# Sorted rows of each image's first half turned by loads and VectorE, image 0's second pair loaded sooner, and two calls of the step loop in another order

## The chip, the cores and the metric

The kernel runs on one core of one Trainium2 chip. A core has five engines that work side by side: TensorE (matrix products; PE in the profile, its weight loads listed apart as PEld), VectorE (DVE), ScalarE (ACT), GpSimd (POOL) and SyncE (SP, which here only starts transfers). Each takes its instructions strictly in the order in which the program lists them for it, and waits on semaphores that other engines or landed transfers raise. Transfers between on-chip memory and HBM are started from a queue (SP's, ACT's or GpSimd's) and carried by 16 DMA engines. The metric is device time in microseconds (us) of one execution; less is better.

## The reference, cut to what matters

x is [4, 32, 128, 128] in f32: four images, regrouped into 128 channels (c) of 4096 pixels (i, j).

```python
# layer 0, for each image: attention between all pairs of pixels
energy = jnp.einsum('bci,bcj->bij', q, q)                      # 4096 x 4096, symmetric
d = jnp.sqrt(jnp.diagonal(energy, axis1=1, axis2=2))
attn = jax.nn.softmax(energy / (d[:, :, None] * d[:, None, :]), axis=-1)
x = gamma * jnp.einsum('bcj,bij->bci', q, attn) + xs           # then put back to image order
# layer 1, on each image's 4096 tokens of 128
t = t + linear_attention(layernorm(t))
n = layernorm(t)
p = softmax(n @ router_w + router_b)                           # 8 experts
top_p, top_i = top_k(p, 2); top_p = top_p / sum(top_p)
t = t + sum_k top_p[k] * (n @ expert_w[top_i[k]] + expert_b[top_i[k]])
```

## The kernel before, in words

**Attention of layer 0 (`attend`).** The 4096 pixels of an image are 8 chunks of 512. Because the energy is symmetric, only the tiles with chunk `jc` <= chunk `i` are computed: a loop over rows `i`, in it over tiles `jc`, in it over four sub-tiles `j` of 128. One turn of the inner loop is a *step*: a product `pe` (L609), its exponential `pr` on ScalarE (L612), and, two steps later, the product `po` (L497, `values`) that multiplies `pr` into the row's output. The tile's mirror image is needed as well. VectorE transposes `pr` in 32x32 blocks into a tile `F` (L421 is the line under which the profile lists it), the queue SP writes F to DRAM (`move`, L530) and reads it back with its groups swapped (`bring`, six transfers, L545), and later four products `pg` (L433, `transposed_share`; L453 for tiles on the diagonal) add it to the other chunk's output. So a usual step on TensorE is pe, po, pg: six instructions of 128x512, since an f32 product takes two.

**What sets the order.** All of it is written out by hand, for TensorE, VectorE, ScalarE and SP. `after(n, f)` puts f in a list that `turn_tick` runs n steps later. `clock` counts TensorE work in units of 128 columns: 2*(CH-c0)/P for a step's pe and po (8 for a full one), 4 for a share. `bring` appends a share to the list `late` with the clock value `clock + LAG` (57) at which it is due, and `step_share` runs one part of the first share that is due. At the end of each step stand `turn_tick()`, then `clock += ...`, then `step_share()`. In the first tile of a row, at j == 2, turn_tick runs the row's first `po`, which needs the accumulator that ScalarE has just copied out for the row before (L502).

**Other work, spread between the steps.** Generators are advanced between steps: `timed` ones at shares of an image's clock (loads and normalisation of the next image's chunk pairs, `prep`), and a `steady` one at most once in 10 clock units (`layer1` of the image before, during `attend` of the next one). A step of the steady generator is two yields.

**The sorted experts (`sorted_experts`, images 0 to 2).** Each half of an image's tokens (h = 0 and 1) is written by GpSimd's indirect transfers to DRAM rows `xs[h]` of 132 values (128 channels and the token's weight), sorted by expert and padded to NT = 39 tiles of 128 rows, each tile of one expert. Then for pairs of tiles (20 of them, one pair in a step): `load` brings the rows to on-chip buffers (SP, L1096); three steps later TensorE turns them with two transposes (L1137) into PSUM, ScalarE copies them out (L1106), in the next step TensorE multiplies them by the expert's matrix, whose place is a register (L1130, two instructions for each tile), VectorE scales the result by the token's weight (L1112), and SP writes it to `ys` (L1116). GpSimd gathers from `ys` afterwards.

**The start.** `prep_first` loads image 0's chunks 0 and 1 (`load_quarters`, L308, into the one buffer `xx`), turns them on VectorE (L316), squares and sums them (L295, L296), takes the power -1/2 on GpSimd (L164), scales (L338), and TensorE transposes them (ptn, L344) into `qn`. `prep(0, 1)` does chunks 2 and 3 in another form: its factors `wide` (L388) are transposed on TensorE (pnorm, L399), and VectorE scales with them. Its load uses the same buffer `xx`.

**The end.** Image 3's layer 1 runs after its attention (`last_parts`).

## Time and profile before

Three runs took 1651.45, 1651.85 and 1653.72 us: the median is 1651.85. The profiled execution took 1650.83 us, with a span of 1649.0 us of instructions and a granted TensorE clock of 0.996.

| What | busy us | share of the span | instructions |
|---|---|---|---|
| TensorE | 1609.9 | 98% | 5192 |
| its weight loads | 846.5 | 51% | 5192 |
| VectorE | 931.5 | 56% | 2383 |
| ScalarE | 898.5 | 54% | 2839 |
| GpSimd | 593.8 | 36% | 565 |

| Group | count | busy us | mean ns of one |
|---|---|---|---|
| po, L497 | 1152 | 549.4 | 559 |
| pe, L609 (128x512, two inputs) | 896 | 458.8 | 594 |
| pg, L433 | 880 | 449.8 | 593 |
| transposes of sorted rows on TensorE, L1137 | 234 | 45.2 | 273 |
| expert products, L1130 | 468 | 71.6 | 275 |
| copies of the turned rows, ScalarE, L1106 | 120 | 45.2 | 377 |
| scaled results, VectorE, L1112 | 120 | 49.9 | 416 |

A busy time is the union of the instructions' spans, and the duration of one matmul holds its way through the array as well: neighbouring matmuls overlap, and what one costs is the distance between the starts of two in a row. The DMA engines moved 345.37 MB in 304297 packets, on average 209 GB/s.

### The profile page before, as it was taken

What the parts mean: (1) busy time and instruction counts of PE and PEld (TensorE: products, weight loads), DVE (VectorE), ACT (ScalarE), POOL (GpSimd) and SP (SyncE); (2) the same over time, 40 slices, a digit from 0 to 9 for tenths busy, and PEclk for the clock granted to TensorE, in tenths of its full rate; (3) what the DMA queues carried; (4) which work ended last, traced back from release to release, by engine and by line L of the source; (5) the groups of instructions that cost most, each with busy time, mean ns of one, the idle gap of its engine ahead of it and who ended that gap; (6) DMA issues with size and microseconds to landing.
All of it is one profiled execution on the core that took longest, in us unless ns stands there. A gap on an engine that the chain in (4) does not pass through costs nothing.

```text
span 1649.0 us, 21309 instructions
## 1 busy us (share of the span) xinstructions
PE 1609.9 (98%) x5192; PEld 846.5 (51%) x5192; DVE 931.5 (56%) x2383; ACT 898.5 (54%) x2839; POOL 593.8 (36%) x565
## 2 busy tenths in 40 slices
PE   8999999999999999999999999999999999999987
PEld 4444544455554455555554455555554455555633
DVE  4543353567586443549478443448658634345786
ACT  3555445466475555547556455556656555545386
POOL 1000000001015441446555543256555652437166
PEclk9999999999999999999999999999999999999999
DMA  4655656676759777997899777798699877886001
GB/s 143 205 179 178 197 187 213 222 231 204 168 196 283 239 222 220 266 257 200 211 221 287 253 236 241 222 268 230 196 209 279 275 248 236 248 251 192 14 14 39
DMA packets 304297, 345.37 MB, mean 209 GB/s; under 512 B 82096, under 2 KB 230704, under 8 KB 289840
## 3 DMA queue, kind: packets, MB, share of 16 engines
q1 hardware_dynamic: 269712, 304.50, 59.9%
q0 software_dynamic: 26624, 25.58, 7.6%
q10 hardware_dynamic: 7840, 13.93, 2.9%
q8 instruction: 44, 0.72, 0.2%
q14 instruction: 77, 0.63, 0.1%
HBM read 167.08 MB, written 182.09 MB: 212 GB/s over the span
## 4 chain that ended last, share of the span: by engine, by line
PE 81%; DVE 7%; DMA 5%; ACT 3%; SPq 2%; issue 1%; POOL 1%; ACTq 0%; DVEq 0%; POOLq 0%
PE po L497 24%; PE pe L609 23%; PE pg L433 20%; PE pys L1130 3%; PE py L1304 3%; PE pg L453 2%; PE pys L1137 2%; PE pgram L725 2%; DMA F<-blocks 1%; DVE F L421 1%; DMA blocks<-rows 1%; SPq L938 1%; ACT pr L612 1%; ACT xn L696 1%; DMA blocks<-F 1%
## 5 line engine op out<-in xcount | busy, mean ns | idle before, releaser
L612 ACT ACTIVATE pr<-pe 128x512 f32<-128x512 f32 (+1 forms) x576 | 322.4, 560 | 547.5 <-PE pe L609 507.0
L497 PE MATMUL po<-pr,qT 128*128 128x512 f32 (+3 forms) x1152 | 549.4, 559 | 4.2 <-ACT o L502 3.9
L609 PE MATMUL pe<-qn,qn 128*128 128x512 f32 x896 | 458.8, 594 | 4.6 <-ACT pr L612 4.6
L433 PE MATMUL pg<-F,qT 128*128 128x512 f32 x880 | 449.8, 593 | 4.7 <-DMA F<-blocks 4.7
L421 DVE STREAM_TRANSPOSE F<-pr 128x512 f32<-128x512 f32 x440 | 305.4, 700 | 134.5 <-ACT pr L612 124.7
L497 PEld LDWEIGHTS po<-pr,qT 128*128 128x128 f32 x1152 | 215.2, 190 | 250.2 <-issue 217.9
L1178 POOL DMA_INDIRECT acc<-ys,place x128 | 202.1, 1579 | 209.1 <-ACT pr L612 134.8
L438 ACT ACTIVATE junk<-F 128x512 bf16<-128x512 f32 x440 | 273.0, 620 | 4.9 <-DMA F<-blocks 4.9
L433 PEld LDWEIGHTS pg<-F,qT 128*128 128x128 f32 x880 | 166.8, 190 | 199.4 <-issue 182.3
L1066 POOL DMA_INDIRECT xs<-xn,place x192 | 186.0, 969 | 184.1 <-ACT pr L612 118.9
L609 PEld LDWEIGHTS pe<-qn,qn 128*128 128x128 f32 x896 | 155.6, 191 | 119.1 <-issue 106.7
L442 DVE TENSOR_TENSOR o<-o,pg 128x512 f32<-128x512 f32 x110 | 75.1, 683 | 205.4 <-PE pg L433 205.2
L1112 DVE TENSOR_TENSOR results<-pys,xn 128x256 f32<-128x256 f32 x120 | 49.9, 416 | 187.2 <-ACT xn L1106 168.5
L164 POOL TENSOR_TENSOR rn<-ss,neg_half 128x8 f32<-128x8 f32 (+1 forms) x17 | 27.2, 1602 | 320.0 <-DVE ss L296 319.9
L612 ACT ACTIVATION_READ_ACCUMULATOR pr<-pe 128x1 f32 x576 | 111.9, 194 | 0.0
L1106 ACT ACTIVATE xn<-pys 128x256 f32<-128x256 f32 x120 | 45.2, 377 | 111.4 <-PE pys L1137 111.4
L1130 PEld LDWEIGHTS pys<-ew_sb,xn 128*128 128x128 f32 x468 | 70.5, 191 | 52.2 <-issue 49.7
L609 PE MATMUL pe<-qn 128*128 128x512 f32 (+3 forms) x256 | 91.4, 440 | 0.7 <-ACT qn L342 0.7
L1178 POOL DMA_INDIRECT yb<-ys,place x64 | 60.8, 950 | 81.1 <-DMA F<-blocks 31.1
L438 ACT ACTIVATION_READ_ACCUMULATOR junk<-F 128x1 f32 x440 | 84.5, 192 | 0.0
L1130 PE MATMUL pys<-ew_sb,xn 128*128 x468 | 71.6, 275 | 0.0
L1304 PE MATMUL py<-ew_sb,xn 128*128 128x512 f32 x128 | 61.5, 622 | 5.1 <-ACT tmp L1260 3.9
(217 smaller groups left out, 1463.2 us busy)
## 6 DMA issues: line engine op xcount, KB each, us to landing
blocks<-F SPq DMA_DIRECT2D x110, 1024.0 KB
F<-blocks SPq DMA_DIRECT2D x220, 192.0 KB
F<-blocks SPq DMA_DIRECT2D x220, 128.0 KB
xn<-xs SPq DMA_DIRECT2D x114, 132.0 KB
ys<-results SPq DMA_DIRECT2D x114, 128.0 KB
F<-blocks SPq DMA_DIRECT2D x220, 64.0 KB
below<-F SPq DMA_DIRECT2D x31, 384.0 KB
T<-in_x_dram SPq DMA_DIRECT2D x64, 128.0 KB
```

Of the source, the lines that this page charges most:

```text
L421: f()
L433: nc.tensor.matmul(pg.rearrange("p (a f) -> p a f", a=4), st["qT"][i][:, ib, :], G[:, :, ib], start=(ib == 0), stop=(ib == NJ - 1),)
L438: nc.scalar.activation(junk, G[:, :, ib], AF.Copy, accum_out=st["sums"][:, NJ * i + ib, jc : jc + 1])
L442: nc.vector.tensor_tensor(st["o"][jc], st["o"][jc], pg, ALU.add)
L497: nc.tensor.matmul(row["po"][:, lo:hi], qT[blk // NJ][:, blk % NJ, :], w, start=start, stop=(row["left"] == 0))
L609: nc.tensor.matmul(pe[:, c0:], qn[jc][:, ts(j, P)], qn[i][:, c0:], start=True, stop=True)
L612: nc.scalar.activation(pr[:, c0:], pe[:, c0:], AF.Exp, accum_out=sums[:, t, i : i + 1]).ins
L1066: inst = nc.gpsimd.indirect_dma_start(xs[h], offset(place[:, i, k : k + 1]), xn[:, k, :], None)
L1112: nc.vector.tensor_tensor(result[:, :n], p[:, 2 * P : 2 * P + n * D].rearrange("p (j c) -> p j c", c=D), bufs[g % 6][:, :n, D : D + 1].to_ ...
L1130: nc.tensor.matmul(p[:, 2 * P + j * D : 2 * P + j * D + D], bufs[6 + g % 2][:, j, :D], weights[:, bass.ds(begins[2 * (g % 2) + j], D)], st ...
L1178: inst = nc.gpsimd.indirect_dma_start(to, None, ys, offset(place[:, i, k : k + 1]), compute_op=op)
L1304: nc.tensor.matmul(bank, xn[:, k, :D], ew_sb[:, 4 * h : 4 * h + 4, :], start=True, stop=True)
```

## The change

**1. First halves.** For h == 0 the rows of a quad of four tiles are loaded by four transfers (one for each 32 channels) that place the 32x32 blocks so that VectorE's blockwise transpose of 128x512 gives the turned rows. TensorE's transposes and ScalarE's copies are gone for this half; TensorE multiplies the four tiles of a quad together, and one VectorE instruction scales them. The weights come by a transfer of their own (`factor`). All buffers are parts of this half's `xn`: two for loads, two for turned rows. The second half (h == 1) is as before.

**2. Image 0's second pair.** It is loaded into a buffer of the pool `work` and no longer into `xx`, directly after the first pair's load and before the tokens `T`. Its four turns stand between the instructions of `prep_first`, whose order on VectorE is now written out, with the first half's sums ahead of the second half's.

**3. The step loop.** `clock` is raised before the two calls, for every step; in the first tile of a row at j == 2, `step_share` runs ahead of `turn_tick`.

**4.** `prep` has one more yield ahead of pnorm for image 0.

```diff
         rows = st["T"][:, ts(kc, 8), :]
         return rows.rearrange("p k (w r) -> p k w r", r=2)
 
-    def load_quarters(b, kc, queues=(nc.sync, nc.sync)):
-
-        xa = xin.tile([P, 2, 2, 2, HW2, 2], F32, tag="xx", name=f"xa_{b}_{kc}")
+    def load_quarters(b, kc, queues=(nc.sync, nc.sync), place=(xin, "xx")):
+
+        xa = place[0].tile([P, 2, 2, 2, HW2, 2], F32, tag=place[1], name=f"xa_{b}_{kc}")
         halves = x[b].rearrange("c (s g) w -> c s (g w)", s=2)
         for a in (0, 2, 1, 3):
             first_row = 16 * kc + 4 * a
...
             )
         return xa
 
+    def turn_quarter(s, k, xa, qT):
+        nc.vector.transpose(
+            qT[:, s, 2 * k : 2 * k + 2, :].rearrange("p h (e r c) -> p r (h e) c", e=2, r=2),
+            xa[:, s, k].rearrange("p r (h t) e -> p (r h) e t", h=2),
+        )
+
     def turn_quarters(s, xa, qT):
         for k in range(2):
-            nc.vector.transpose(
-                qT[:, s, 2 * k : 2 * k + 2, :].rearrange("p h (e r c) -> p r (h e) c", e=2, r=2),
-                xa[:, s, k].rearrange("p r (h t) e -> p (r h) e t", h=2),
-            )
+            turn_quarter(s, k, xa, qT)
 
     def prep_first(st):
 
...
         yield
         ss = stat.tile([P, 2 * NJ], F32, tag="ss", name=f"ss_{b}_{kc}")
         rn = stat.tile([P, 2 * NJ, 1], F32, tag="rn", name=f"rn_{b}_{kc}")
-        for s in range(2):
+        def rows_squared(s):
             turn_quarters(s, xa, qT)
-            squares(b, kc, s, qT, ss)
+            sq = work.tile([P, NJ, P], F32, tag="qs", name=f"sq_{b}_{kc}_{s}", bufs=2)
+            nc.vector.tensor_tensor(sq, qT[:, s], qT[:, s], ALU.mult)
+            return sq
+
+        def summed(s, sq):
+            nc.vector.tensor_reduce(ss[:, ts(s, NJ)], sq, AX.X, ALU.add)
             pow_neg_half(rn[:, ts(s, NJ), 0], ss[:, ts(s, NJ)])
-        keep_running(40, ps_g, "pg")
-        scaled = []
-        for s in range(2):
-            qs = work.tile([P, NJ, P], F32, tag="qs", name=f"qs_{b}_{kc}_{s}", bufs=2)
+
+        def scale_rows(s):
+            qs = work.tile([P, NJ, P], F32, tag="grp", name=f"qs_{b}_{kc}_{s}", bufs=2)
             nc.vector.tensor_tensor(qs, qT[:, s], rn[:, ts(s, NJ)].to_broadcast([P, NJ, P]), ALU.mult)
             scaled.append(qs)
+
+        scaled = []
+        keep_running(40, ps_g, "pg")
+        summed(0, rows_squared(0))
+        sq = rows_squared(1)
+        st["turns"].pop(0)()
+        scale_rows(0)
+        summed(1, sq)
+        st["turns"].pop(0)()
+        st["turns"].pop(0)()
+        scale_rows(1)
+        st["turns"].pop(0)()
         for s, qs in enumerate(scaled):
             qn = channels(b, kc, s, st)
             pt, done = hold(f"ptn_{b}_{kc}_{s}", lambda p, qn=qn: nc.scalar.activation(qn, p, AF.Copy))
...
 
 
 
-        ahead = 2 if b == 0 and kc == 1 else 5
-        xa = load_quarters(b, kc)
+        soon = b == 0 and kc == 1
+        ahead = 2 if soon else 5
+        if soon:
+            xa = load_quarters(b, kc, place=(work, "wide"))
+            yield
+        else:
+            xa = load_quarters(b, kc)
         if b == 0:
             load_tokens(st["T"][:, ts(kc, 8), :], b, 8 * kc, 8)
             xx = rows_of_image(b, kc, st)
-        for _ in range(ahead):
-            yield
         qT = chunks_of(b, kc, st)
-        for s in range(2):
+        if soon:
+            st["turns"] = [partial(turn_quarter, s, k, xa, qT) for s in range(2) for k in range(2)]
+            yield
+        for _ in range(0 if soon else ahead):
+            yield
+        for s in range(0 if soon else 2):
             turn_quarters(s, xa, qT)
             yield
         if b > 0:
...
         for s in range(2):
             nc.vector.tensor_copy(wide[:, :, s], rn[:, ts(s, NJ)].to_broadcast([P, NJ, 64]))
         yield
-        if b:
-            yield
+        yield
 
         def scale_all(bank):
             for s in range(2):
...
                     elif jc == i and j in (1, 2):
 
                         after(1 if j == 2 and order[-1] == i else 2, partial(below, own, (2, 1) if j == 1 else (3,)))
-                    turn_tick()
                     clock[0] += 2 * (CH - c0) // P
-                    step_share()
+                    steps = (turn_tick, step_share)
+                    for step in reversed(steps) if jc == order[0] and j == 2 else steps:
+                        step()
                     yield
 
     def finish():
...
                         nc.tensor.transpose(p[:, ts(j, P)], bufs[g % 6][:, j, :D], ident)
                 return done
 
+            room = xn[:, half, :].rearrange("p k w -> p (k w)")
+            parts = [room[:, 4 * DW * i : 4 * DW * i + 4 * D] for i in range(4)]
+            quads = [(g, min(4, NT - 4 * g)) for g in range((NT + 3) // 4)]
+
+            def read(inst):
+                wait_for(inst.ins, xs_made[h], "a tile holds tokens of any row")
+                xs_read[h].append(inst.ins)
+
+            def load_blocks(g, n):
+                rows = xs[h][4 * g * P : (4 * g + n) * P, :D].rearrange("(m i) w -> i m w", i=S)
+                for q in range(4):
+                    read(
+                        nc.sync.dma_start(
+                            parts[g % 2][ts(q, S), : n * D].rearrange("i (m c) -> i m c", c=S), rows[:, :, ts(q, S)]
+                        )
+                    )
+
+            def turn(g, n):
+                nc.vector.transpose(parts[2 + g % 2][:, : n * D], parts[g % 2][:, : n * D])
+
+            def four_products(factor, g, n):
+
+                def leave(p):
+                    result = keep["results"].rearrange("p g j c -> p (g j) c")[:, ts(g % 2, 4)]
+                    nc.vector.tensor_tensor(
+                        result[:, :n], p[:, : n * D].rearrange("p (j c) -> p j c", c=D),
+                        factor[:, 4 * g : 4 * g + n].to_broadcast([P, n, D]), ALU.mult,
+                    )
+                    nc.sync.dma_start(
+                        ys[4 * g * P : (4 * g + n) * P, :].rearrange("(j p) d -> p j d", p=P), result[:, :n]
+                    )
+
+                p, done = hold(f"pys_{b}_{h}_{g}", leave)
+                _, begins = nc.values_load_multi_w_load_instructions(
+                    begin[0:1, h, 4 * g : 4 * g + n], engines=[mybir.EngineType.PE], min_val=0,
+                    max_val=(E - 1) * D,
+                    skip_runtime_bounds_check_because="D times a count of at most E - 1, never negative",
+                )
+                weights = ew_sb.rearrange("p e c -> p (e c)")
+                for j in range(n):
+                    nc.tensor.matmul(
+                        p[:, ts(j, D)], parts[2 + g % 2][:, ts(j, D)],
+                        weights[:, bass.ds(begins[j], D)], start=True, stop=True,
+                    )
+                return done
+
+            def turned_by_vector():
+
+                factor = stat.tile([P, NT, 1], F32, tag="factor", name=f"factor_{b}_{h}", bufs=1)
+                read(nc.sync.dma_start(factor, xs[h].rearrange("(t p) w -> p t w", p=P)[:, :, D : D + 1]))
+                leaves = {}
+                for at in range(4 * len(quads) + 10):
+                    for first_at, act in (
+                        (8, turn), (0, load_blocks), (11, partial(four_products, factor)), (13, lambda g, n: leaves.pop(g)()),
+                    ):
+                        if at >= first_at and (at - first_at) % 4 == 0 and (at - first_at) // 4 < len(quads):
+                            g, n = quads[(at - first_at) // 4]
+                            made = act(g, n)
+                            if first_at == 11:
+                                leaves[g] = made
+                    yield
+
             if "results" not in keep:
                 keep["results"] = work.tile([P, 4, 2, D], F32, tag="df", name=f"results_{b}", bufs=1)
-            done = None
             begins = []
-            for at in range(len(pairs) + 5):
-                if at < len(pairs):
-                    load(*pairs[at])
+
+            def turned_by_tensor():
+
+                done = None
+                for at in range(len(pairs) + 5):
+                    if at < len(pairs):
+                        load(*pairs[at])
+                    if done:
+                        done()
+                    yield
+                    turned, applied = (pairs[at - d] if 0 <= at - d < len(pairs) else None for d in (3, 4))
+                    done = products(turned, applied) if turned or applied else None
+                    yield
                 if done:
                     done()
-                yield
-                turned, applied = (pairs[at - d] if 0 <= at - d < len(pairs) else None for d in (3, 4))
-                done = products(turned, applied) if turned or applied else None
-                yield
-            if done:
-                done()
+
+            yield from (turned_by_tensor if h else turned_by_vector)()
             if h == 1:
                 st["sorted"] = True
             yield from idle(1)
...
     UNITS = 3 * NJ * NJ * NCH * (NCH - 1) // 2 + 7 * NJ * NCH
 
     first, second = prep_first(states[0]), prep(0, 1, states[0])
-    next(first)
-    load_weights()
+    ordered = ExitStack()
     next(first)
     next(second)
+    load_weights()
+    ordered.enter_context(tc.manual_schedule(engines=ENGINES))
+    next(second)
+    next(first)
     load_tokens(states[0]["T"][:, 0:8, :], 0, 0, 8)
-
-    ordered = ExitStack()
-    ordered.enter_context(tc.manual_schedule(engines=ENGINES))
-    timed = [(first, 0, 1, 2), (second, 0.5, 5.5, 10)]
+    next(second)
+    next(second)
+    timed = [(first, 0, 1, 2), (second, 1.3, 5.5, 8)]
     for b in range(B):
 
         if b == 0:
```

More of the change, by code (lines that the diff above doesn't have):

```diff
@@ L356, in prep @@
             xx = rows_of_image(b, kc, st)
-        for _ in range(ahead):
+        qT = chunks_of(b, kc, st)
+        if soon:
+            st["turns"] = [partial(turn_quarter, s, k, xa, qT) for s in range(2) for k in range(2)]
             yield
-        qT = chunks_of(b, kc, st)
-        for s in range(2):
+        for _ in range(0 if soon else ahead):
+            yield
+        for s in range(0 if soon else 2):
             turn_quarters(s, xa, qT)
```

## The prediction

> **What bounds the kernel now.** First the page's busy times and the chain that ended last:
>
> ```profile
> PE 1609.9 (98%) x5192; PEld 846.5 (51%) x5192; DVE 931.5 (56%) x2383; ACT 898.5 (54%) x2839; POOL 593.8 (36%) x565
> PE 81%; DVE 7%; DMA 5%; ACT 3%; SPq 2%; issue 1%; POOL 1%; ACTq 0%; DVEq 0%; POOLq 0%
> ```
>
> TensorE sets the time: what leaves its queue or its gaps is gained, unless another engine comes to hold it up. But a busy share is no price, so next I read TensorE's timeline inside a first half's expert products (start, length, instruction, count):
>
> ```profile
> 601.98 0.61 PE L1130 MATMUL pys<-ew_sb,xn 128*128 x4
> 602.42 0.38 PE L1137 MATMUL pys<-ident,xn 128*128 128x128 f32 x2
> 602.64 1.02 PE L609 MATMUL pe<-qn,qn 128*128 128x512 f32 x2
> 603.50 1.02 PE L497 MATMUL po<-pr,qT 128*128 128x512 f32 x2
> ```
>
> Starts tell the price: two transposes take 602.42 to 602.64, so 0.11 us each, as each of the four product instructions does ((602.42 - 601.98)/4); two of 128x512 take 0.86. By these distances TensorE loses only some 62 us of the span in gaps: 10 in the first 50 us, 20 after 1500, and 31 between, of three kinds here. A start wait, a row start and a late F:
>
> ```profile
> 19.73 0.38 PE L497 MATMUL po<-pr,qT 128*128 128x128 f32 x2
> 22.50 0.66 PE L399 MATMUL pnorm<-ident,wide 128*128 128x128 f32 x4 [2.39 <-DVE wide L388]
> 570.49 1.02 PE L609 MATMUL pe<-qn,qn 128*128 128x512 f32 x2
> 571.70 1.13 PE L497 MATMUL po<-pr,qT 128*128 128x512 f32 x2 [0.18 <-ACT o L502]
> 572.66 1.02 PE L433 MATMUL pg<-F,qT 128*128 128x512 f32 x2
> 850.92 1.10 PE L433 MATMUL pg<-F,qT 128*128 128x512 f32 x2 [1.79 <-DMA F<-blocks]
> ```
>
> A gap is longer than its bracket, since the pipeline drains too: po would have started at 570.49 + 0.86 = 571.35, so 0.35 is lost at this row start. Nineteen row starts lose 0.35 (three of them 0.67): 7.2 us. The late F's are three: 1.16 us at 184, 1.95 at 851, 2.04 at 1240. Last the room of the others, by stage (stretch, length, busy time of PE, PEld, DVE, ACT, POOL; clock, DMA share, GB/s):
>
> ```profile
> 583.00:640.00 57.00, 57.00 (x213) 32.00 (x212) 23.37 (x44) 29.82 (x91) 21.31 (x23) 1.00 0.73 226
> 640.00:720.00 80.00, 79.82 (x290) 44.12 (x289) 35.27 (x70) 41.22 (x128) 29.65 (x19) 1.00 0.89 246
> ```
>
> The first is a first half, the second mostly the second half beside the gathers. TensorE loses nothing in the first, and next to nothing at a DMA share of 0.89.
>
> **What the Trainium skill says.** "TensorE: Matmul & The Clock Gate", Part 4: PE-mode transpose, gives about 275 ns for a 128x128 transpose in a kernel. The trace's 273 ns agree as a duration, but the 0.11 us between starts is the cost. "VectorE: DVE Perf Modes", The three transpose paths: VectorE turns 32x32 blocks only; hence the load that places the blocks. The kernel does this already (L950, 128x512: 0.70 us). "DMA: Bandwidth & Descriptors", Specifications: below 512 B a transfer isn't at line rate. The trace's 128 B packets took 15.2 ns in the mean and its 528 B ones 32.2: half the rate.
>
> **The change part by part.** *First halves, TensorE.* Three images x 39 transposes x 0.11 = 12.9 us less; the 117 products stay, and the register loads are as many. ScalarE loses 60 copies of 0.377 (22.6 us): worth nothing by itself, ScalarE has room. VectorE gets 30 turns x 0.70 = 21 us, and 30 scalings of 128x512 (nearest row, L442, 0.683: 20.5) for 60 of 0.416 (25): +5.5 us in each stretch of 57 with 23.4 busy. TensorE's 57 us cover it; uncovered it would cost those 5.5 a half.
>
> *First halves, transfers.* A half has 4992 rows. Before: 4992 packets of 528 B x 32.2 = 161 us of one DMA engine; after: 19968 of 128 B x 15.2 = 303, and 4992 four-byte weights (nearest: the trace's 4 B packets, 10.8 ns: 54). That is +196, or 12.2 us of all sixteen: the share of 0.73 becomes about 0.94. SP's issue times (min/median/max ns):
>
> ```profile
> L938 SPq DMA_DIRECT2D blocks<-rows x48: 557/744/3385, 413.5 to 1228.8; - x48
> L1096 SPq DMA_DIRECT2D xn<-xs x120: 338/424/2255, 571.4 to 1465.6; - x120
> ```
>
> The new loads have 512 pieces each, between 256 (L1096) and 1024 (L938). A quad costs SP 4 x (0.42 to 0.74) + one store of 0.39 = 2.1 to 3.4 us, before 2 x 0.42 + 2 x 0.39 = 1.6. Four steps (two quads, 6.04 us each: 5.16 for pe, po, pg twice and 0.88 for eight products) also hold one F (2.7 + 0.4): SP is then busy for 7.3 to 9.9 of 12.1 us. F has room: in this stretch it landed, by its 2 KB packets, 9 us or more before its share.
>
> The new wait is VectorE's turn on its load. Behind it in the queue stand the F transposes, scalings and sums; late F transposes hold the six pr buffers, then the exponentials, then pe. The load buffers are two, so load g+2 starts when turn g is done, and must land by turn g+2, 12.1 us later: issue at most 3, landing some 3 to 5 (F's own: about 3 after its last issue), being queued behind an F 0 to 3. That makes 6 to 11 us, so it fits, with 1.5 steps more ahead of the product. I charge 1.5 us in all for bursts (bounds: a gain of 0, as pr's six buffers may swallow all; a loss of 25, the rival below).
>
> *The start.* The second pair's load waits today for the first pair's turns (SP's four start at 7.67). Now it stands right behind the first's: started from about 2.1 to 4.6, landed 3.3 later (the first pair: last start 2.35, turned at 5.62), so at 7.9, wanted at about 8.8. VectorE's sum of the first half stands ahead of the second half's turns: 8.21 becomes 7.6, rn 9.71 becomes 9.1, ptn 0.5 us earlier. Then VectorE: scale, sum, two turns (11.3), scale at 11.75 to 12.45, turn, two squares and two sums (2.7) to 15.5, GpSimd's power 1.6, wide 0.5: 17.7, where pnorm's turn on TensorE comes at 19.4. The gap ahead of pnorm (22.50 - 19.95 = 2.55) goes. Sum 3.0; bounds 0 (load late, each us late also delays the scale in front of TensorE's first product) and 3.5 (the added yield may remove a smaller pnorm gap of 0.4).
>
> *The step loop.* Raising clock first means that `bring` reads a value 8 higher: each share falls due one step (1.72 us of pe and po, with 8 units) later. In the changed order of TensorE's instructions this undoes the swap: in rows 3 to 7 of every image no share is due at j == 2 any more, it comes at j == 3. Only rows 1 and 2 of images 1 to 3 have a share ahead of their first po, and these six lost nothing before. So the swap itself is worth 0. The delay is worth more: the late F's of 1.16, 1.95 and 2.04 shrink by 1.72 each, 4.6 us. F is held a step longer, of six buffers some five in use. Four row starts (row 7 of images 1 and 2, row 0 of 2 and 3) get products between the old row's last po and the new one's first: 1.0 us. From image 3's last row, fourteenth step on, TensorE's order is unchanged, and image 2's second half ends four steps earlier before it, so the end keeps its length.
>
> *Sum.* 1650.83 (profiled, span 1649.0) - 12.9 - 3.0 - 4.6 - 1.0 + 1.5 = 1630.8; the median of the runs stands 1.0 above the profiled execution: 1632.
>
> **The rivals.** *Swap works as labelled*, or bursts cost nothing and the end gets shorter: up to 7.2 - 1.0 more, 1625. For it: the gaps are there; against it: the order. *Only the transposes pay*: the second pair lands late, other late F's replace the old: 1652 - 12.9 + 1.5 = 1641. For it: DMA at 0.94. *No change*: what TensorE sheds comes back as waits, 1651; against it: distances of 0.11 are seen in full while nothing waits. *Slower*: the load loop. Place: VectorE's turn in first halves. If turn g to turn g+2 takes longer than 12.1 us, VectorE falls behind by the excess 5 times a half, 15 times in all, and nothing absorbs a steady excess. 20 us of gains are gone at 20/15 = 1.4 us over, a loop of 13.5 us; at 15 us it costs 43 us: 1675. For it: share 0.94, SP near 80%, F loads ahead in the same queue; against it: the 0.89 stretch without gaps, and my 6 to 11 us.
>
> **How the numbers follow.** Forecast 0.69 (own range 1627 to 1637); only transposes, or the loop just touched (1637 to 1647) 0.12; swap works (1622 to 1627) 0.08; no change 0.03; slower (1656 to 1690) 0.08. Range 1625 to 1643. A measurement tells 0.2%, 3.3 us, from no change: faster 0.89, same 0.03, slower 0.08.
>
> **What would show it.** Right: 117 transposes on TensorE instead of 234; starts 0.11 apart in the products; pnorm without a gap; row starts in rows 3 to 7 still losing 0.35; gaps from late F gone at the old places; VectorE's turns waiting for loads only here and there. Wrong: TensorE idle released by VectorE's turned rows or by ScalarE's exponentials in the first halves, F later than its share there, or the start later because the first scale waits for the second pair.

## The result, and the profile after

The changed kernel takes 1643.57 us (median of 6 runs, 1640.39 to 1646.9), the kernel before 1651.28 on the same chip (1649.4 to 1653.72): a ratio of 0.9953, with a 95% interval of 0.9941 to 0.9965. That is 7.7 us faster; the forecast was 20 us, and the time lies just above the top of the range, 1643. The profiled execution took 1644.21 us, its span 1642.4, 6.6 less than the span before.

The page's busy times and the chain that ended last, of the changed kernel:

```profile
PE 1600.1 (97%) x5075; PEld 834.0 (51%) x5075; DVE 945.8 (58%) x2383; ACT 877.3 (53%) x2779; POOL 592.7 (36%) x565
PE 81%; DVE 8%; DMA 4%; ACT 2%; SPq 2%; issue 1%; POOL 1%; ACTq 0%; DVEq 0%; POOLq 0%
```

117 instructions have left TensorE, which still sets the time. But its busy time fell by 9.8 us (from 1609.9) and the span by only 6.6 (from 1649.0): it does less, and waits more. In the chain VectorE has 8% for 7% before; that is a hint, no more, since the page gives whole points.

Next, the expert products of a first half. TensorE's timeline (start, length, instruction, count):

```profile
600.00 1.06 PE L1207 MATMUL pys<-ew_sb,xn 128*128 x8
600.89 1.02 PE L635 MATMUL pe<-qn,qn 128*128 128x512 f32 x2
```

No transpose stands between the products any more, and 8 product instructions take 600.00 to 600.89, the same 0.11 each. The stages of that stretch (busy time of PE, PEld, DVE, ACT, POOL; clock, DMA share, GB/s):

```profile
583.00:640.00 57.00, 57.00 (x193) 30.54 (x192) 30.76 (x52) 24.78 (x79) 18.00 (x20) 1.00 0.92 258
640.00:720.00 80.00, 80.00 (x284) 43.69 (x283) 36.55 (x71) 42.11 (x130) 37.28 (x24) 1.00 0.88 242
```

The DMA share rose from 0.73 to 0.92 and VectorE's work from 23.4 to 30.8 us, and TensorE loses nothing to either. At the start, pnorm:

```profile
19.75 0.38 PE L523 MATMUL po<-pr,qT 128*128 128x128 f32 x2
19.98 0.60 PE L425 MATMUL pnorm<-ident,wide 128*128 128x128 f32 x4
20.41 1.02 PE L635 MATMUL pe<-qn,qn 128*128 128x512 f32 x2
```

The gap of 2.55 ahead of it is gone. So the 12 us that are missing lie elsewhere. The groups of TensorE's instructions give the lead (busy and mean; after the last bar the idle time ahead of the group, and who ended it):

```profile
L523 PE MATMUL po<-pr,qT 128*128 128x512 f32 (+3 forms) x1152 | 549.8, 559 | 2.9 <-ACT o L528 2.9
L635 PE MATMUL pe<-qn,qn 128*128 128x512 f32 x896 | 459.1, 594 | 8.6 <-ACT pr L638 8.6
L459 PE MATMUL pg<-F,qT 128*128 128x512 f32 x880 | 449.6, 592 | 2.0 <-DMA F<-blocks 1.9
L798 PE MATMUL pbd<-ident,rdx 128*128 128x128 f32 x64 | 9.9, 277 | 5.6 <-DVE rdx L776 5.5
```

The same four in the kernel before:

```profile
L497 PE MATMUL po<-pr,qT 128*128 128x512 f32 (+3 forms) x1152 | 549.4, 559 | 4.2 <-ACT o L502 3.9 <-DMA F<-below 0.2 <-DMA F<-blocks 0.2
L609 PE MATMUL pe<-qn,qn 128*128 128x512 f32 x896 | 458.8, 594 | 4.6 <-ACT pr L612 4.6
L433 PE MATMUL pg<-F,qT 128*128 128x512 f32 x880 | 449.8, 593 | 4.7 <-DMA F<-blocks 4.7
L771 PE MATMUL pbd<-ident,rdx 128*128 128x128 f32 x64 | 9.6, 273 | 0.1
```

The row starts (po) and the late F's (pg) lose less, as forecast. New are 5.5 us in which pbd waits for VectorE's rdx, and 4.0 more in which pe waits for ScalarE's exponentials.

The same account in full, by the distances between starts, as the prediction counted: each matmul is priced at its own back-to-back distance (0.429 us for 128x512, 0.110 for 128x128), and what a distance exceeds that is lost. All in us, with the number of gaps; the last three columns are experiments told below. The first two columns are traces from one chip, the last three from two others, where the kernel before took 1653.8, 1653.8 and 1650.8 us for 1651.3 here.

| | before | after | step loop alone | old step order | LAG 49 |
|---|---|---|---|---|---|
| matmuls at their own distance | 1584.7 | 1571.8 | 1584.7 | 1571.8 | 1571.8 |
| lost up to 26 us | 9.4 | 6.8 | 8.1 | 5.4 | 5.3 |
| row starts | 7.2 (18) | 5.2 (14) | 5.2 (14) | 7.2 (18) | 0.4 (1) |
| shares with a late F | 5.2 (3) | 2.1 (1) | 2.8 (2) | 3.6 (3) | 7.6 (3) |
| pbd waits for rdx | 0 | 6.3 (5) | 6.8 (5) | 0 | 0 |
| pe waits for pr | 5.1 (3) | 9.5 (5) | 9.0 (5) | 5.1 (3) | 5.1 (3) |
| matmuls at about double distance | 0 | 1.5 | 3.2 | 0 | 1.5 |
| other gaps over 0.25 | 1.3 | 1.3 | 4.0 | 2.3 | 2.2 |
| gaps under 0.25 | 6.3 | 7.9 | 7.9 | 6.5 | 4.9 |
| from 1500 us on | 20.1 | 20.2 | 19.8 | 18.6 | 18.7 |
| span (with 9.8 outside the matmuls) | 1649.0 | 1642.4 | 1661.4 | 1630.3 | 1627.5 |
| stretches at half clock: up to 26 us, between, from 1500 us on | 1, 0, 2 | 1, 1, 2 | 0, 2, 1 | 0, 0, 1 | 0, 1, 1 |

From before to after: 12.9 of transposes, 2.6 at the start, 3.1 of late F's and 2.0 of row starts are gained, 20.6 together, very nearly the forecast; and 6.3 + 4.3 + 1.5 + 1.6 = 13.7 are lost in four rows in which the forecast had no loss.

The last row counts the stretches of 3.41 us in which the trace has a granted clock of 0.50, without the one that ends every trace. In the middle they are the matmuls at double distance. At the start one costs about 1.4 us with the same code: 6.8 against 5.4 (changed kernel, old step order), 9.4 against 8.1 (before, step loop alone). So the old order's and LAG 49's smaller losses up to 26 us are no gain of theirs, and those from 1500 us on may not be one either. What decides on such a stretch stands in the last section.

**Where pbd waits.** It turns 1/sum of an image's rows, and stands a fixed number of yields behind den (the sums) and rdx, which VectorE makes. The kernel before at the end of image 1 (timeline):

```profile
770.09 0.82 PE L453 MATMUL pg<-F,qT 128*128 128x256 f32 x4
771.42 2.77 DVE L372 TENSOR_TENSOR qn<-xx,pnorm 64x512 f32<-64x512 f32 x4
774.23 0.23 DVE L744 TENSOR_REDUCE den<-sums 128x8 f32<-128x72 f32 x1
774.73 0.78 DVE L749 TENSOR_SCALAR rdx<-rd,gam 128x256 f32<-128x256 f32 x2
776.13 0.60 PE L771 MATMUL pbd<-ident,rdx 128*128 128x128 f32 x4
```

The changed kernel at the same place:

```profile
767.03 0.82 PE L479 MATMUL pg<-F,qT 128*128 128x256 f32 x4
767.35 2.76 DVE L399 TENSOR_TENSOR qn<-xx,pnorm 64x512 f32<-64x512 f32 x4
770.13 0.87 DVE L810 BATCH_NORM_STATS2 bs_a<-T 128x6 f32<-128x128 f32 x4
772.62 0.56 DVE L488 TENSOR_TENSOR o<-o,pg 128x384 f32<-128x384 f32 x1
773.09 0.22 DVE L771 TENSOR_REDUCE den<-sums 128x8 f32<-128x72 f32 x1
773.58 0.62 DVE L776 TENSOR_SCALAR rdx<-rd,gam 128x256 f32<-128x256 f32 x2
774.25 0.66 PE L798 MATMUL pbd<-ident,rdx 128*128 128x128 f32 x4 [1.67 <-DVE rdx L776]
```

The first line of each is the last share that the image's rows wait for. Before, it ended ahead of the next image's scaling (L372), den came right behind that scaling, and rdx was ready at 775.51, with 0.6 us to spare. After, the share comes two of the short steps at a row's end later in TensorE's order, the scaling only one: the share's sum on VectorE (L488) and with it den have slid behind the scaling (L399), the statistics of other rows (L810), six small operations and a transpose. VectorE works without a pause from 765.3 to 774.2. TensorE on the other hand has less between the share and pbd, and would have reached pbd at 772.41 (774.25 less the gap of 1.84).

**Where pe waits.** ScalarE's normalising (L723) stands in its queue ahead of an exponential, and waits for GpSimd's nbo, which waits for VectorE's statistics. The kernel before has this wait too (timeline):

```profile
1261.18 1.02 PE L609 MATMUL pe<-qn,qn 128*128 128x512 f32 x2
1262.99 1.65 ACT L696 ACTIVATE xn<-T,nbo,rsf 128x128 f32<-128x128 f32 x4 [3.81 <-POOL nbo L692]
1265.26 1.12 PE L609 MATMUL pe<-qn,qn 128*128 128x512 f32 x2 [1.56 <-ACT pr L612]
```

The changed kernel:

```profile
1255.13 1.02 PE L635 MATMUL pe<-qn,qn 128*128 128x512 f32 x2
1255.66 1.67 POOL L164 TENSOR_TENSOR rsf<-dm_f,neg_half 128x8 f32<-128x8 f32 x1 [6.12 <-DVE sv_f L715]
1257.70 0.27 POOL L719 TENSOR_SCALAR nbo<-nbf 128x8 f32<-128x8 f32 x1
1258.00 1.65 ACT L723 ACTIVATE xn<-T,nbo,rsf 128x128 f32<-128x128 f32 x4 [3.81 <-POOL nbo L719]
1259.56 0.57 ACT L638 ACTIVATE pr<-pe 128x512 f32<-128x512 f32 x1
1260.27 1.38 PE L635 MATMUL pe<-qn,qn 128*128 128x512 f32 x2 [2.40 <-ACT pr L638]
1261.44 1.91 PE L523 MATMUL po<-pr,qT 128*128 128x512 f32 x2
```

ScalarE idles for 3.81 us in both, with an exponential behind the wait. But its normalising comes 2.87 us after TensorE's last pe, before 1.81 us; TensorE stops for 2.57 us, before for 1.72, and then goes at half clock (the two of po take 1.71 from start to start instead of 0.86). The stop near 872 has grown in the same way, from 1.72 to 2.58. Two more stops, of 1.32 and 1.52 us near 840 and 1228, are new: ScalarE's wait for nbo there was 1.27 and 0.87 us and is 4.68 and 4.85. These four make up the 4.3 us (a fifth stop, near 486, shrank by 0.2). The link from the shares to these statistics isn't followed instruction by instruction here; that the shares' due time makes the loss is what the experiments show. The Trainium skill, "TensorE: Matmul & The Clock Gate", Part 1, says that ScalarE and VectorE take their queues strictly in order; this case agrees, for the exponential at 1259.56 stood behind those 3.81 us.

### The profile page after: what moved, and what is told of

Its sections match the earlier page's. It is cut to its first block, busy times and chain, and to the rows that moved or that the text cites. A ratio compares the mean times of both kernels' runs of the same rounds, so it can differ in the third digit from the quotient of the medians.

```text
span 1642.4 us, 20931 instructions
## 1 busy us (share of the span) xinstructions
PE 1600.1 (97%) x5075; PEld 834.0 (51%) x5075; DVE 945.8 (58%) x2383; ACT 877.3 (53%) x2779; POOL 592.7 (36%) x565
## 4 chain that ended last, share of the span: by engine, by line
PE 81%; DVE 8%; DMA 4%; ACT 2%; SPq 2%; issue 1%; POOL 1%; ACTq 0%; DVEq 0%; POOLq 0%
PE po L523 24%; PE pe L635 23%; PE pg L459 20%; PE py L1398 3%; PE pg L479 2%; PE pys L1207 2%; PE pys L1157 1%; PE pgram L752 1%; DMA F<-blocks 1%; SPq L965 1%; DVE F L447 1%; DVE bs_f L989 1%; PE pys L1164 1%; DMA acc<-t 1%; ACT xn L723 1%
## 5 line engine op out<-in xcount | busy, mean ns | idle before, releaser
L723 ACT ACTIVATE xn<-T,nbo,rsf 128x128 f32<-128x128 f32 x128 | 54.1, 494 | 38.7 <-POOL nbo L719 38.7
L1139 DVE TENSOR_TENSOR results<-pys,xn 128x256 f32<-128x256 f32 (+1 forms) x60 | 24.9, 415 | 82.5 <-ACT xn L1133 71.2
L164 POOL TENSOR_TENSOR rsa<-dm_a,neg_half 128x8 f32<-128x8 f32 x16 | 26.5, 1654 | 117.1 <-DVE sv_a L715 117.0
L164 POOL TENSOR_TENSOR rsf<-dm_f,neg_half 128x8 f32<-128x8 f32 (+1 forms) x15 | 26.2, 1750 | 114.0 <-DVE sv_f L715 114.0
```

The costliest lines, as they stand in the source:

```text
L164: pinned(nc.gpsimd.tensor_tensor(dst, src, neg_half.to_broadcast(list(src.shape)), ALU.pow))
L723: nc.scalar.activation(xn[:, k, :D], T[:, k, :], AF.Identity, scale=rs[:, k, :], bias=nb[:, k, :])
```

## The experiments

The theory (A): part 3, the step loop, raises the clock ahead of turn_tick, so that every share falls due 8 units, one step, late. The late F's gain by it, but the closing work of an image, which needs the shares, and VectorE's and ScalarE's queues behind it lose more. The main rival (B): the turned first halves disturb what comes after them. All times are compared with the kernel before on the same chip, since chips differ (before took 1650.8 to 1662.6 us), so the ratios count; a gain in us is the ratio's share of the time of before there.

**The old step order in the changed kernel**

```
-                    clock[0] += 2 * (CH - c0) // P
-                    steps = (turn_tick, step_share)
-                    for step in reversed(steps) if jc == order[0] and j == 2 else steps:
-                        step()
+                    turn_tick()
+                    clock[0] += 2 * (CH - c0) // P
+                    step_share()
```

> The changed kernel with the step order of before (turn_tick, clock raised, step_share), the other three parts kept. Theory A, the raised clock costs more than it brings: the waits of pbd for VectorE's rdx (6.3 us in the changed kernel) go, TensorE's waits for ScalarE's pr fall from 9.5 back to about 5.1, four matmuls at double length (1.5) go, and the late F's come back (3.1): 1644 - 6.3 - 4.4 - 1.5 + 3.1 = 1635, some 16 below the kernel before. Rival B, the turned first halves disturb the steps after them (scatters, gathers, stores): the waits stay and the time is 1641 to 1646.

Measured 1633.12 against 1653.78: ratio 0.9881 (0.9867 to 0.9895), 19.7 us faster. By the table the waits of pbd and the two new waits of pe are gone, and the two long ones are back at 1.7. Without its part 3 the change brings what was forecast for the whole of it; A holds, B falls.

**The changed step loop alone, in the kernel before**

```
-                    turn_tick()
-                    clock[0] += 2 * (CH - c0) // P
-                    step_share()
+                    clock[0] += 2 * (CH - c0) // P
+                    steps = (turn_tick, step_share)
+                    for step in reversed(steps) if jc == order[0] and j == 2 else steps:
+                        step()
```

> The kernel before with the changed step loop alone (clock raised ahead of turn_tick, share first in a row's first tile). The prediction's step: 5.6 us faster than before. Theory A: the late F's give 3, waits of pbd and of ACT's normalise take 6 to 12: 3 to 9 us slower than before. Rival B, these waits come only with the turned first halves: 3 to 6 us faster than before.

Measured 1662.37 against 1653.78: ratio 1.0053 (1.0041 to 1.0065), 8.8 us slower, at the top of A's estimate. (By the two traces, from two chips, it is 12.4.) The five waits of pbd and the five of pe are there without a turned first half or a new start, so they belong to the step loop alone. The prediction gave this step 5.6 us of gain.

**The clock really kept**

```
+                    if jc == order[0] and j == 2:
+                        was = clock[0]
+                        clock[0] += 2 * (CH - c0) // P
+                        step_share()
+                        now, clock[0] = clock[0], was
+                        turn_tick()
+                        clock[0] = now
+                    else:
+                        turn_tick()
+                        clock[0] += 2 * (CH - c0) // P
+                        step_share()
```

> The changed kernel with the clock really kept: deferred work sees the clock unraised in every step, and in a row's first tile the share is issued ahead of the deferred products. 29 of the 32 rows then have a share ahead of their first po (in the changed kernel 6, in the kernel before none). Theory A: as the old step order, without the 0.35 us at 19 row starts: 1635 - 7 = 1628. Rival B, as above: 1634 to 1640. Rival C, the row starts are not a matter of order, or the moved share's F is late: 1633 to 1637, no better than the old step order.

Measured 1629.26: ratio 0.985 (0.9836 to 0.9863), 24.8 us faster than before and some 5 more than with the old step order. The row starts fall from 7.2 us to 0.35, so the swap can pay, 6.8 us; but the moved shares wait longer for their F (3.6 becomes 7.5, of it 3.84 and 2.87 in row 4 of images 2 and 3), and 1.6 goes to matmuls at half clock. It ends between A's 1628 and C.

**One number: LAG 49 for 57 in the changed kernel**

```
-    LAG = 57
+    LAG = 49
```

> The changed kernel with one number changed: LAG 49 for 57, so that a share falls due at the old clock again in spite of the raise (29 of 32 rows then have a share ahead of their first po). Theory A, all the loss is that each share comes 8 units late: as the kernel with the clock kept, 0.984 to 0.987 of before, 22 to 27 us faster. Rival, it is the raise itself or the code around it: 0.994 to 0.997, as the changed kernel.

Measured 1627.0 against 1650.76: ratio 0.9854 (0.9841 to 0.9867), 24.1 us faster, as with the clock kept. All code of part 3 stays, only the 8 units are taken back, and the whole loss is gone. The groups of TensorE's instructions in this kernel, to be held against the four above:

```profile
L523 PE MATMUL po<-pr,qT 128*128 128x512 f32 (+3 forms) x1152 | 548.2, 558 | 0.2 <-ACT o L528 0.2
L635 PE MATMUL pe<-qn,qn 128*128 128x512 f32 x896 | 459.4, 594 | 4.6 <-ACT pr L638 4.6
L459 PE MATMUL pg<-F,qT 128*128 128x512 f32 x880 | 449.6, 592 | 7.1 <-DMA F<-blocks 7.1
L798 PE MATMUL pbd<-ident,rdx 128*128 128x128 f32 x64 | 9.6, 273 | 0.1
```

And a row start in its timeline, then the dearest cost of the swap that is left there:

```profile
563.00 1.02 PE L635 MATMUL pe<-qn,qn 128*128 128x512 f32 x2
563.86 1.02 PE L459 MATMUL pg<-F,qT 128*128 128x512 f32 x2
564.72 1.02 PE L523 MATMUL po<-pr,qT 128*128 128x512 f32 x2
...
1219.29 1.02 PE L635 MATMUL pe<-qn,qn 128*128 128x512 f32 x2
1223.03 1.10 PE L459 MATMUL pg<-F,qT 128*128 128x512 f32 x2 [2.71 <-DMA F<-blocks]
```

The share now stands between the row's third pe and its first po, and the starts are 0.86 apart. The same row start in the changed kernel:

```profile
569.38 1.02 PE L635 MATMUL pe<-qn,qn 128*128 128x512 f32 x2
570.59 1.13 PE L523 MATMUL po<-pr,qT 128*128 128x512 f32 x2 [0.18 <-ACT o L528]
```

No share there, and 1.21 between pe and po, 0.35 too many: what the prediction said of rows 3 to 7. By the traces 29 of 32 rows have a share ahead of their first po with LAG 49, 6 in the changed kernel, none before.

**The raise without the swap**

```
-                    for step in reversed(steps) if jc == order[0] and j == 2 else steps:
+                    for step in steps:
```

> The changed kernel without its swap: the clock raised ahead of turn_tick in every step, the share never ahead of the deferred products. By the prediction's step the swap is worth 0, since with the clock raised only six rows have a share there: the time of the changed kernel, 0.995 of before (7 to 9 us faster than before). Rival, those six rows hold the loss: 15 us faster than before or more.

Measured 1646.2 against 1650.76: ratio 0.9966 (0.9953 to 0.9979), 5.6 us faster. Its interval overlaps that of the changed kernel (0.9941 to 0.9965). The two ratios are 2 us apart, with 0 inside the margin (-1 to 5), and by its trace the same 14 row starts lose 5.2 us: no gain of the swap, as it was made, can be seen, and the loss isn't in it.

**Half a step of lateness, in the kernel with the clock kept**

```
-    LAG = 57
+    LAG = 61
```

> The kernel with the clock kept, shares due half a step later (LAG 61 for 57). Theory A, in degrees: late F's of row 4 smaller (3.8 and 2.9 by about 0.9 each), a part of the waits of pbd and pr back: 0.985 to 0.991 of before. Rival, lateness costs nothing until a whole step: 0.982 to 0.985.

Measured 1636.82: ratio 0.9915 (0.9902 to 0.9928), 14 us faster. Half the lateness gives back 11 us of the kept clock's 25, a little more than expected: pbd waits for 3.2 us in three places and pe for 6.2; seven rows have lost their share again, and row starts cost 3.4. Unlike expected, the late F's did not shrink: 8.4 us, of it 3.04 at 1217 where the trace names no cause.

**The turned first halves alone, in the kernel before** (with the functions that this line calls)

```
+            yield from (turned_by_tensor if h else turned_by_vector)()
```

> The kernel before with the first halves' sorted rows turned by loads and VectorE, and nothing else. By the prediction's step: 3 x 39 transposes x 0.11 = 12.9 us faster, less at most 1.5 for bursts: 1638 to 1640. Theory A agrees, with no burst: 1638. Rival B: 1644 to 1650, the gain is given back in waits after the first halves.

Measured 1636.95 against 1653.78: ratio 0.9905 (0.9892 to 0.9919), 15.7 us faster, of which the trace shows 12.2 in its span: 12.9 of transposes, less 0.6 in gaps. Nothing is given back later.

**The new start alone, in the kernel before** (with prep and prep_first of the change)

```
+    next(second)
     load_weights()
...
-    timed = [(first, 0, 1, 2), (second, 0.5, 5.5, 10)]
+    timed = [(first, 0, 1, 2), (second, 1.3, 5.5, 8)]
```

> The kernel before with the new start alone (second pair loaded sooner, its turns placed between the first pair's work, one more yield ahead of pnorm). By the prediction's step: 3.0 us faster than before, of it 2.55 the gap ahead of pnorm. Theory A agrees: 2.6 to 4.0 faster. Rival: the first product comes later, nothing gained, within 1 us of before.

Measured 1658.39 against 1662.57: ratio 0.9974 (0.9962 to 0.9986), 4.3 us faster (2.3 to 6.3); the loss up to 26 us falls from 9.4 to 5.2. Some 1.3 of that is the stretch at half clock, which this trace lacks; against the trace of the step loop alone, which lacks it too (8.1), it is 2.9. Both parts together are 20.0 by these two runs, 19.7 by the old step order: they add up.

**The two waits taken one by one in the changed kernel.** Two more yields ahead of pbd in close_rows, and in another kernel two more ahead of the normalising in attention_rows:

```
             if not last_rows:
                 yield
                 yield
+                yield
+                yield
             pb, done = hold(f"pbd_{b}_{kc}", divide)
```

> The changed kernel with two more yields between den and pbd in close_rows, so one more step of TensorE's work between the sums and what turns them. Theory A: the five waits of pbd for rdx (6.3 us) go and nothing else: 1643.6 - 6.3 = 1637. Rival, the stages behind are a step later and wait in its place: 1640 to 1646.

Measured 1653.7 against 1662.57: ratio 0.9948 (0.9927 to 0.9968), no better than the changed kernel. The waits of pbd are not gone: three of 2.0, 2.7 and 2.3 us for five of 6.3 in all. In its timeline den stands behind yet another set of statistics (770 to 776.9) and TensorE waits for rdx until 778.1. The trace shows one gain, and what it is spent on: the two new stops of pe are gone and the long ones short again (5.1 in three places), but the row starts cost 7.6, and two more stops of pe near 1323 and 1328, of a kind told below, 4.2. Moving the reader doesn't help when the writer is moved by the same stream and queues on the busiest helper; my expectation A was wrong here.

```
             nc.sync.dma_start(t2[:, ts(u, 8)], T[:, ts(u, 8), :])
             yield
+            yield
+            yield
```

> The changed kernel with two more yields ahead of the normalising in attention_rows, so that GpSimd's nbo is there when ScalarE comes to it. Theory A: TensorE's five waits for pr (9.5 us) and the four matmuls at double length (1.5) go: 1643.6 - 11 = 1633. Rival B, what holds pr is the load of ScalarE itself and not its wait for GpSimd: 1641 to 1645.

Measured 1652.63 against 1662.57: ratio 0.9938 (0.9916 to 0.996). All five waits of pe at the old places are gone, so they hung on the normalising, as theory A has it; the time, 10 us below before, is nevertheless rival B's. Its timeline at the place shown above:

```profile
1254.81 1.02 PE L635 MATMUL pe<-qn,qn 128*128 128x512 f32 x2
1255.11 1.65 ACT L723 ACTIVATE xn<-T,nbo,rsf 128x128 f32<-128x128 f32 x4 [2.78 <-POOL nbo L719]
1257.38 1.13 PE L635 MATMUL pe<-qn,qn 128*128 128x512 f32 x2
```

ScalarE still waits, but a step later, when no exponential is due behind it: 2.57 between the two pe, the distance of a full step. The time shows little of it, for two reasons: pbd's waits grew to 9.2 us, and near 1320 to 1335 us TensorE lost 9.5 us in a stall of another kind and the two stretches at half clock behind it:

```profile
1327.54 0.60 ACT L638 ACTIVATE pr<-pe 128x512 f32<-128x512 f32 x1 [6.56 <-remote]
1327.60 0.69 DVE L468 TENSOR_TENSOR o<-o,pg 128x512 f32<-128x512 f32 x1 [6.49 <-remote]
```

ScalarE and VectorE stop together and nothing in the trace holds them. The four kernels that ran together on this chip, and the last one below, have such a stall, of 2 to 6 us, between 1306 and 1328 us; the others have none. What it is stays open. The kernel before took 11 us longer on this chip than on the first, but no trace of it from here was kept, so whether it stalls too isn't known; that makes the whole times of these five, and their ratios, less telling than their traces.

**Row 4 in the old order.** Where the moved share waits for its F longest (row 4 of images 1 to 3), the share was put back behind the products, once with the clock kept and once with LAG 49:

```
-                    if jc == order[0] and j == 2:
+                    if jc == order[0] and j == 2 and not (b > 0 and i == 4):
```

```
-                    for step in reversed(steps) if jc == order[0] and j == 2 else steps:
+                    for step in reversed(steps) if jc == order[0] and j == 2 and not (b and i == 4) else steps:
```

> The kernel with the clock kept (1629.3), but in row 4 of images 1 to 3 with the old order, where the moved share waited 3.84 and 2.87 us for a late F and four matmuls ran at double length afterwards. Theory: the late F's fall back to about 1.6 and 1.2, so 4 to 5.5 us faster than with the clock kept in every row: 1624 to 1626. Rival, the stall only moves on to the next share: 1628 to 1631.

> The changed kernel with LAG 49, and in row 4 of images 1 to 3 the share behind the deferred products as before. Theory: of the 6.5 us that the moved shares of these rows wait for their F some 3 to 4 go, so 0.982 to 0.984 of before, 27 to 30 us faster. Rival, the wait moves to the next share: 0.985 to 0.987, as with LAG 49 alone.

Measured 1636.64 against 1662.57, ratio 0.9836 (0.9811 to 0.9862), and 1634.69 against 1662.48, ratio 0.9834 (0.9813 to 0.9855). The late F's fall to 4.1 and 4.3 us from 7.5 and 7.6, about as expected, but the intervals overlap those of the kernels without the exception (0.985 and 0.9854): the two can't be told apart. All four versions beat both kernels; LAG 49 does it with one number.

## Why the prediction was wrong, point by point

- **First halves, TensorE** (12.9 us): right. The account has 12.9, part 1 alone measured 15.7 (13.4 to 17.9).
- **First halves, transfers** (share 0.73 to 0.94, issue and landing 6 to 11 us of 12.1, 1.5 us for bursts): right in the mechanism, the charge was too high by all of it. The share is 0.92. From a turn to the start of the load that takes its buffer 0.7 to 4.7 us pass, from there to landing 3.2 to 6.3 in the steady loop, at most 9.3 together; by its packets every load landed 2.5 us or more ahead of its turn, and VectorE never waited. SP's issue took 0.49 us in the median, as bounded:

```profile
L1179 SPq DMA_DIRECT2D xn<-xs x120: 302/488/5631, 558.4 to 1376.1; - x120
```

  The rival *slower* is refuted with that.
- **The start** (3.0 us): right; 2.6 in the changed kernel, 4.3 alone (2.9 by traces with the same clock).
- **The gaps before**: two counts were off, with little weight in the sum. The row starts that lose time are eighteen, not nineteen (7.2 us is the sum of eighteen), and between 50 and 1500 us TensorE loses 25 us by the account above, not 31. More telling is a kind of gap that the list left out: pe's three waits for ScalarE's exponentials, 5.1 us in the kernel before. They were the sign that the normalising reached TensorE already, and they grew.
- **The step loop, the swap** (worth 0, since in rows 3 to 7 no share is due at j == 2): right for the code as it stands (26 of 32 rows without a share, and no gain of the swap to be seen). The rival *swap works as labelled* is refuted for this kernel and true of the one with LAG 49.
- **The step loop, the delay** (the late F's shrink, 4.6, and four row starts get work, 1.0): the step that failed. Its two terms are nearly right in sum, 3.1 and 2.0; the row starts are the four that it named, twice as dear. What it left out, and so put at nothing, is the other side of a delay: it followed F, the share's input, which had become less late, and not the share's result. The sums and o of an image wait for the last shares, and den, pbd, the statistics and the normalising stand behind them in queues that VectorE, ScalarE and GpSimd share with the step loop. With the stretch at half clock and the small gaps that took 13.7 us: 6.3 at pbd, 4.3 at pe, 1.5 and 1.6. Alone the step measured 8.8 us slower, a whole 14 away from its 5.6 faster; in the changed kernel it costs 12.
- Of the late F's the first did not shrink but grew, from 1.16 to 2.10. Its six loads were issued from 173.1 to 177.3 and landed at 181.7; why that late was not settled. It goes with the raise: 1.8 to 2.3 us in the five traces with shares a step late, 1.7 with half a step, 0.6 to 1.2 in the other eight.
- **The end keeps its length**: right, 20.1 and 20.2.
- The rival *only the transposes pay*, 1641, came nearest in time, by luck: it had the second pair land late and other late F's under a fuller DMA, and the second pair did not, and F's waits fell by 3.1.

The prediction's own sum without the step loop would have been 1637.4 (1631.8 + 5.6); that kernel ran 19.7 us below before, which on the first chip is 1631.6. The forecast 1632 came out where it did because a gain of 5.6 that isn't there stood in for gains of the other parts that were set too low (14.4, measured 19.7). In the two traces about 3 us of that are two stretches at half clock, which the old step order's lacks and before's has; how often the other runs have them isn't known.

## What to carry to other kernels

A piece of work that is put off has two ends: ask what its input gains, and then who reads its result, how far behind that reader stands in program order, and what shares the reader's queue. When a planner counts in a clock, a line moved across the clock's step shifts every due time; compare the order before and after, and take the shift back with the planner's own constant before judging the rest. And do not move a reader by yields when its writer hangs on the same stream: both move.

## What the runs showed of the hardware that was not expected

- The matmuls at double distance are a granted clock of 0.50, and not every stop of TensorE is followed by it. The changed kernel at its stops of 2.57 us (ended at 1260.27) and 2.58 us (ended at 872.51); columns as for the stages above:

```profile
1257.60:1261.01 3.41, 1.00 (x3) 0.49 (x3) 3.17 (x16) 3.01 (x9) 0.51 (x3) 1.00 1.04 401
1261.01:1264.42 3.41, 3.41 (x5) 1.33 (x4) 2.39 (x6) 3.41 (x11) 0.00 (x0) 0.50 0.66 198
868.48:871.89 3.41, 1.62 (x4) 0.38 (x2) 3.21 (x15) 1.65 (x5) 1.79 (x4) 1.00 0.94 300
```

  In each of the fourteen traces the changes of the clock lie on one grid of 3.41 us. The first stop falls into one stretch of the grid, in which TensorE idles for 2.67 us in all (by distances); the clock is at half in the next. The second is split by the edge at 871.89 and leaves 1.96 us idle in the fuller stretch; the clock stays. So it is throughout, between 26 and 1500 us: after each of the 13 stretches at full clock with 2.22 us of idle time or more the clock was at half, after none with 2.11 or less. The stop of 3.84 us in the kernel with the clock kept is split into 2.00 and 1.91, and nothing followed. The Trainium skill, "TensorE: Matmul & The Clock Gate", Part 1, gives an idle window of about 3.4 us, free-running, after which the clock falls to half. The length and the fixed grid agree; but here a window need not be idle from end to end, 2.2 of its 3.41 us were enough. Where the grid lies differs from run to run, so a stop of one length can be followed by a loss of about 1.5 us in one run and not in another: the stop near 1260 was not, with 2.56 us, in the kernel without the swap.
- A DMA share of 0.92 over 57 us, with 60% of its packets of 128 B (23% of the packets' time), cost TensorE nothing. Loads of 512 pieces took SP 0.49 us to issue in the median, against 0.42 for loads of 256, and the load of 4992 single words only 0.38 (three issues of 0.382 to 0.388): the time did not follow the number of pieces.
